# Block 1 of a four-block kernel: where the value matmuls stand, which engine makes a norm's products, and one beat for the next layer's features

## The chip, the cores and the metric

The kernel runs on one core of one Trainium2 chip. The metric is the device time of one execution, in microseconds. A profile adds the span from the first to the last instruction and the time of every instruction on each engine: PE (TensorE) for matmuls and transposes, ACT (ScalarE), DVE (VectorE), POOL (GpSimd), and SP, which issues the DMAs.

## What is computed

The program runs four blocks one after the other on an input of 2 batches x 1024 rows x 128 columns. The change touches only block 1, a two-layer attention block with two heads of 64:

```
def layer(x):                               # 2 layers; x: (2, 1024, 128)
    xl = ln(x) * g1 + b1
    q, k, v = xl @ wq + bq, xl @ wk + bk, xl @ wv + bv      # 2 heads of 64
    q, k = rotary(q), rotary(k)
    x = x + (softmax(q @ k.T / 8) @ v) @ wo
    hid = (ln(x) * g2 + b2) @ w1 + bias     # 128 -> 512
    return x + (hid * sigmoid(1.702 * hid)) @ w2
x = x0 + layers(layernorm(x0))
```

`ln` and `layernorm` take a row's mean and variance: (x - mean) / sqrt(var + 1e-5).

## The kernel before, in words

**Tiles.** Block 1 (class BlockA) works on tiles of 128 query rows: 2 layers x 2 batches x 8 tiles = 32 tiles. A tile is named here by its place in that order, 0 to 31. Four tiles make a group, and a group of 512 rows is the unit of the norms, the projection and the two-matmul feed-forward part.

**Beats.** The order of the work is written out by hand. Every tile has eight beats. A step is put down as "so many beats from now, at this rank"; when a beat comes, its steps run in order of rank and issue their instructions. Each engine takes its instructions strictly in the order in which they were issued. Steps of a chain are put down when the step before them has run; the ones with a set of allowed beats (EARLY is 1, 2, 3, 5 of the eight, LATE is 4, 5, 6, 7) take the first allowed beat that no such step has taken.

**A tile's own steps** (`tile`): the scores S at beat 0 (L372: eight matmul instructions into two wide PSUM tiles, then two maxima on DVE, L378); the two exponentials on ACT at beats 3 and 4 (L384); four groups of four transposes, T00, T10, T01, T11, at beats 9 to 12, that is beats 1 to 4 of the next tile (L395). ACT copies T00 and T10 out of PSUM (L398), DVE copies T01 and T11 (L400). The value matmuls come in two halves of 16 instructions, V0 at beat 13 and V1 at beat 15 (L407); `keep` at beat 16 copies their result on ACT (L415).

**A group's steps** (`after`, put down when the fourth tile is kept): the projection (L442) with two divisions on DVE (L450) and two additions on POOL (L454); a norm; `turn`, four transposes (L345) and one ACT copy with scale and bias, hT (L346); four `up` steps (L467, then tanh on ACT L470, a small POOL step L473 and, two beats later, a DVE step L475); two `down` steps (L488). In layer 0 a group then prepares layer 1 (`prep`): a norm, `features` (again four transposes, L345, and hT on ACT, L346), keys (L314, then ACT L316 and POOL L317), queries (L321, DVE L322) and values (L329, DVE L334).

**The norm** (`norm`) has two steps. `stats` at beat 0, 5 or 7, rank -2, is four pairs of DVE instructions (L289, L290). `product` one beat later, rank 0, is on POOL: add epsilon (L293), power -0.5 (L294), negate the mean (L295), and then four products (x - mean) * rs, one for each 128x128 tile (L297). For the very last group these four are on DVE. A norm is made 17 times by this function: four times for batch 1 at the start (two for the outer layernorm, two for layer 0), four times for layer 1, eight times in `after`, and once near the end for block 2.

**PSUM.** The two wide score tiles s0 and s1 take four of the eight banks. Everything else shares four banks, tag "bank": each group of transposes, the projection's two tiles, features, keys, queries, values, ups, downs, and the value matmuls' result u, which is held from V0 until `keep`.

**The order around the change.** In tile 10 (second group of batch 0, layer 0; the same order comes in tiles 14, 18 and 22) the steps that reach PE and ACT are, before the change:

```
tile 9,  beat 4: T11, PROJECT      beat 5: V0, features (next layer)   beat 7: V1
tile 10, beat 0: keep, product (POOL), S    beat 1: T00, keys   beat 2: T10
         beat 3: exp, T01    beat 4: exp, T11, queries   beat 5: V0, TURN
         beat 6: values      beat 7: V1, up0
```

The groups of tiles 6, 26 and 30 have a norm and a `turn` at the same beats, but no `prep` beside them.

Of the kernel before, what the change touches and what calls it, by code (L numbers as in the profile page):

```python
# [24 lines left out]
AF = mybir.ActivationFunctionType  # L25
ALU = mybir.AluOpType
# [82 lines left out]
class Pipe:  # L109
# [6 lines left out]
    def later(self, beats, f, bank=False, rank=0):  # L116
        at = self.now + beats
        if bank:
            among = range(1, 8) if bank is True else bank
            while at in self.taken or at % 8 not in among:  # L120
                at += 1
            self.taken.add(at)
        self.due.setdefault(at, []).append((rank, f))
# [54 lines left out]
class BlockA:  # L178
# [102 lines left out]
    def norm(self, src, dst, beats, eng=None):  # L281

        k, nc = self.k, self.k.nc
        st, mv, rs = self.small("st", [4, 6]), self.small("mv", [4, 2]), self.small("rs", [4])
        mn = self.small("mn", [4])

        def stats():
            for i in range(4):
                nc.vector.bn_stats(st[:, i, :], src[:, i, :])  # L289
                nc.vector.bn_aggr(mv[:, i, :], st[:, i, :])  # L290

        def product():
            nc.gpsimd.tensor_scalar(rs, mv[:, :, 1], 1e-5, None, ALU.add)  # L293
            nc.gpsimd.tensor_tensor(rs, rs, k.mhalf[:, :4], ALU.pow)  # L294
            nc.gpsimd.tensor_scalar(mn, mv[:, :, 0], -1.0, None, ALU.mult)  # L295
            for i in range(4):
                (eng or nc.gpsimd).tensor_scalar(  # L297
                    dst[:, i, :], src[:, i, :], mn[:, i : i + 1], rs[:, i : i + 1], ALU.add, ALU.mult
                )

        return (beats, (0, 5, 7), stats, -2), (1, False, product, 0)
# [46 lines left out]
    def prep(self, l, b, g):  # L348
        xn = self.p3.tile([P, 4, D], F32, tag="xn", name=self.k.name("xn"))
        features, keys, queries, values = self.linears(l, b, g, xn)  # L350
        return (
            *self.norm(self.x(b, g), xn, 1), (5, self.EARLY, features, 5), (2, self.EARLY, keys, 5),
            (1, self.LATE, queries, 5), (1, self.LATE, values, 5),
        )

    def tile(self, l, b, qt):
        k, nc = self.k, self.k.nc
        q, kk, v = self.q[b], self.kk[b], self.v[b]
        later = self.pipe.later
        g = qt // 4  # L360
        st = self.st.setdefault((l, b, g), {})
        cut = slice(qt % 4 * P, qt % 4 * P + P)
        t = {}

        def score():
            assert ("ready", l, b, 1) in self.st or (l, b) == (0, 0)
            t["s"] = [k.ps_a.tile([P, S], F32, tag=f"s{h}", name=k.name("s")) for h in range(2)]
            for j in range(2):
                for h in range(2):
                    rows = slice(h * 64, (h + 1) * 64)  # L370
                    keys = slice(j * 512, (j + 1) * 512)
                    nc.tensor.matmul(  # L372
                        t["s"][h][:, keys], q[rows, qt * P : (qt + 1) * P], kk[rows, keys],
                        start=True, stop=True,
                    )
            t["nm"] = [self.small("nm", [1]) for _ in range(2)]
            for h in range(2):
                nc.vector.tensor_reduce(t["nm"][h], t["s"][h], AX.X, ALU.max, negate=True)  # L378

        def exp(h):  # L380
            if qt % 4 == 0 and h == 0:
                st["sums"] = self.p2.tile([P, 2, 4], F32, tag="sums", bufs=3, name=k.name("sums"))
            t["pr", h] = self.p2.tile([P, S], F32, tag="pr", bufs=4, name=k.name("pr"))
            nc.scalar.activation(  # L384
                t["pr", h], t["s"][h], AF.Exp, bias=t["nm"][h],
                accum_out=st["sums"][:, h, qt % 4 : qt % 4 + 1],
            )

        def turn(h, j):
            if h == j == 0:  # L390
                t["pT"] = self.p2.tile([P, 2, MT, P], F32, tag="pT", name=k.name("pT"))
            ps = self.bank()
            for i in range(4):
                at = (j * 4 + i) * P
                nc.tensor.transpose(ps[:, i * P : (i + 1) * P], t["pr", h][:, at : at + P], k.ident)  # L395
            dst = t["pT"][:, h, j * 4 : j * 4 + 4].rearrange("p i q -> p (i q)")
            if j == 0:
                nc.scalar.copy(dst, ps)  # L398
            else:
                nc.vector.tensor_copy(dst, ps)  # L400

        def value(j):
            if j == 0:
                t["u"] = self.bank()
            for kb in range(j * 4, j * 4 + 4):
                for h in range(2):
                    nc.tensor.matmul(  # L407
                        t["u"][h * 64 : h * 64 + 64, :P], v[:, kb, h * 64 : h * 64 + 64],
                        t["pT"][:, h, kb], start=(kb == 0), stop=(kb == MT - 1),
                    )  # L410

        def keep():
            if qt % 4 == 0:
                st["us"] = self.p2.tile([P, 512], F32, tag="us", name=k.name("us"))
            nc.scalar.copy(st["us"][:, cut], t["u"][:, :P])  # L415
            if qt % 4 == 3:
                self.after(l, b, g, st)

        for at, rank, f in (
            (0, 0, score), (3, 0, lambda: exp(0)), (4, 0, lambda: exp(1)), (9, 2, lambda: turn(0, 0)),  # L420
            (10, 2, lambda: turn(1, 0)), (11, 2, lambda: turn(0, 1)), (12, 2, lambda: turn(1, 1)),
            (13, 2, lambda: value(0)), (15, 2, lambda: value(1)), (16, -3, keep),
        ):
            later(at, f, rank=rank)

# [1822 lines left out]
```

## Time and profile before

| what | us |
|---|---|
| median of 3 runs | 1286.3 (1286.21 to 1288.46) |
| the profiled execution | 1286.38 |
| its span, first to last instruction | 1284.6 |
| PE busy | 1147.2 (89%) |
| DVE busy | 874.7 (68%) |
| ACT busy | 645.9 (50%) |
| POOL busy | 488.7 (38%) |

Block 1 takes roughly the first 340 us. Times in the trace are microseconds from the span's start. A line of the timeline has the start, the duration, the engine, the source line and operation, what it writes and reads, how many instructions were merged, and in square brackets how long the engine was idle before it and what released it. "PEld" is the weight load that goes ahead of each matmul. "PEclk" is the clock that TensorE was granted, as a share of full speed.

### The profile page before, as it was taken

The page shows a single profiled execution, that of the slowest core. Times are in us where ns is not written, and L with a number is a line of the kernel's source. Part 1 is how long each engine was busy: PE and PEld are TensorE (multiplying, and loading weights), DVE is VectorE, ACT ScalarE, POOL GpSimd, SP SyncE. Part 2 cuts the span into 40 slices and gives each one's busy share as a digit, 9 for nine tenths or more (in the row PEclk, how much of TensorE's full clock was granted, in tenths as well). Part 3 has the DMA queues.
Part 4 walks back from the last instruction along what each step waited for, and adds up shares of the span by engine and source line. Part 5 has one row for each costly group of instructions (what it writes and reads, how often), then busy time and mean ns, then how long its engine had stood idle before and what let it go on. Part 6 is the DMA issues. An engine that isn't in the chain of part 4 may idle for free.

```text
span 1284.6 us, 23479 instructions
## 1 busy us (share of the span) xinstructions
PE 1147.2 (89%) x9441; PEld 744.3 (58%) x9441; DVE 874.7 (68%) x1782; ACT 645.9 (50%) x1216; POOL 488.7 (38%) x565
## 2 busy tenths in 40 slices
PE   5899999999688989989989877989999978997798
PEld 3566666666356656656656634545555543433688
DVE  5566666555587776776777525556577989999763
ACT  5455455444355665665664545656766754441000
POOL 1523333232588776676677442212222211100000
PEclk9999999999899999999999988989998999999799
DMA  9000000000010000010100011000000000000000
GB/s 296 3 1 1 1 1 1 2 1 1 18 26 22 22 22 18 22 26 18 26 22 18 5 50 69 2 1 2 2 1 1 2 1 1 0 17 1 26 17 17
DMA packets 19840, 25.18 MB, mean 20 GB/s; under 512 B 2762, under 2 KB 13716, under 8 KB 19476
## 3 DMA queue, kind: packets, MB, share of 16 engines
q1 hardware_dynamic: 19076, 23.02, 6.5%
q8 instruction: 75, 1.23, 0.4%
q10 hardware_dynamic: 656, 0.66, 0.2%
q14 instruction: 33, 0.27, 0.1%
HBM read 13.32 MB, written 1.05 MB: 11 GB/s over the span
## 4 chain that ended last, share of the span: by engine, by line
PE 60%; DVE 24%; ACT 7%; POOL 5%; issue 4%; DMA 0%; DVEq 0%; POOLq 0%; ACTq 0%
PE big L1667 6%; PE mm L1750 5%; PE bank L407 4%; PE s L372 4%; PE bank L962 4%; PE s L727 3%; PE bank L882 2%; PE s L1264 2%; PE s L837 2%; PE bank L467 2%; PE tr L1301 2%; PE s L1260 2%; DVE nm L1269 2%; PE bank L488 2%; DVE nm L378 2%
## 5 line engine op out<-in xcount | busy, mean ns | idle before, releaser
L1269 DVE TENSOR_REDUCE nm<-s 128x4 f32<-128x1024 f32 (+1 forms) x64 | 71.0, 1151 | 58.8 <-PE s L1264 58.5
L378 DVE TENSOR_REDUCE nm<-s 128x1 f32<-128x1024 f32 x64 | 75.1, 1215 | 51.9 <-PE s L372 51.9
L1302 ACT COPY pT<-tr 128x512 f32<-128x512 f32 x120 | 70.0, 598 | 71.8 <-PE tr L1301 71.6
L774 POOL TENSOR_TENSOR t<-raw,tab 128x512 f32<-128x512 f32 x62 | 77.2, 1267 | 74.4 <-DVE raw L765 74.4
L1301 PE MATMUL tr<-ident,pr 128*128 128x128 f32 x480 | 77.1, 284 | 2.6 <-ACT pT L1302 2.3
L736 ACT ACTIVATE sq<-s 128x1024 f32<-128x1024 f32 x32 | 32.8, 1023 | 87.0 <-PE s L727 87.0
L384 ACT ACTIVATE pr<-s,nm 128x1024 f32<-128x1024 f32 x64 | 71.0, 1120 | 7.9 <-DVE nm L378 7.8
L781 POOL TENSOR_TENSOR raw<-raw,tab 128x1024 f32<-128x1024 f32 x31 | 73.1, 2360 | 2.4
L788 POOL TENSOR_TENSOR raw<-raw,t 128x1024 f32<-128x1024 f32 x31 | 73.2, 2361 | 1.7
L395 PEld LDWEIGHTS bank<-ident,pr 128*128 128x128 f32 x512 | 56.2, 141 | 30.0 <-issue 22.5
L407 PE MATMUL bank<-pT,v 128*64 128x128 f32 x1024 | 72.5, 286 | 0.7 <-DVE pT L400 0.2
L1676 ACT ACTIVATE hid<-big,cols 128x512 f32<-128x512 f32 x62 | 41.9, 687 | 59.3 <-PE big L1667 59.3
L1667 PE MATMUL big<-xTd,d_gate 128*128 128x512 f32 x128 | 66.9, 611 | 5.0 <-DVE r_above L1917 2.5
L1667 PE MATMUL big<-xTd,d_up 128*128 128x512 f32 x128 | 68.5, 626 | 2.7 <-DVE r_above L1914 2.0
L407 PEld LDWEIGHTS bank<-pT,v 128*64 128x64 f32 x1024 | 57.2, 141 | 22.1 <-issue 10.8
L398 ACT COPY pT<-bank 128x512 f32<-128x512 f32 x64 | 34.9, 588 | 68.3 <-PE bank L395 68.3
L1301 PEld LDWEIGHTS tr<-ident,pr 128*128 128x128 f32 x480 | 54.6, 144 | 21.1 <-issue 11.7
L372 PE MATMUL s<-kk,q 64*128 64x512 f32 x256 | 64.7, 615 | 0.6 <-ACT pr L384 0.5
L395 PE MATMUL bank<-ident,pr 128*128 128x128 f32 x512 | 65.2, 276 | 0.0
L727 PE MATMUL s<-b_wqkv,hT 128*128 128x512 f32 x128 | 62.8, 613 | 1.7 <-ACT hT L694 1.3
L1750 PEld LDWEIGHTS mm<-d_down,hid 128*128 128x128 f32 x496 | 60.8, 195 | 5.7 <-DVE xo L1781 1.9
L1750 PE MATMUL mm<-d_down,hid 128*128 128x128 f32 x496 | 61.5, 279 | 1.3 <-DVE xo L1781 1.3
(368 smaller groups left out, 2833.8 us busy)
## 6 DMA issues: line engine op xcount, KB each, us to landing
vs<-v SPq DMA_DIRECT2D x60, 130.0 KB, 2.2
b_wqkv<-in_L_ffn_wqkv_dram SPq DMA_DIRECT2D x2, 768.0 KB, 9.4
b_tab<-in_c_xpos_dram SPq DMA_DIRECT2D x1, 1024.0 KB, 9.0
d_up<-in_L_ffn_Wup_dram SPq DMA_DIRECT2D x1, 1024.0 KB, 7.2
d_gate<-in_L_ffn_Wgate_dram SPq DMA_DIRECT2D x1, 1024.0 KB, 9.2
out_dram<-xo SPq DMA_DIRECT2D x3, 256.0 KB, 2.3
rows<-in_rows_dram SPq DMA_DIRECT2D x1, 760.0 KB, 6.6
b_w<-in_L_ffn_w_dram SPq DMA_DIRECT2D x2, 341.0 KB, 7.3
```

The source lines that it names most:

```text
L372: nc.tensor.matmul(t["s"][h][:, keys], q[rows, qt * P : (qt + 1) * P], kk[rows, keys], start=True, stop=True,)
L378: nc.vector.tensor_reduce(t["nm"][h], t["s"][h], AX.X, ALU.max, negate=True)
L395: nc.tensor.transpose(ps[:, i * P : (i + 1) * P], t["pr", h][:, at : at + P], k.ident)
L407: nc.tensor.matmul(t["u"][h * 64 : h * 64 + 64, :P], v[:, kb, h * 64 : h * 64 + 64], t["pT"][:, h, kb], start=(kb == 0), stop=(kb == MT - 1),)
L727: nc.tensor.matmul(qk[:, cut], lhsT, k.b_wqkv[:, l, cut], start=True, stop=True)
L774: nc.gpsimd.tensor_tensor(t2[:, :, :, a : a + 32], r4[:, :, :, z : z + 32], tab(1)[:, :, None, a : a + 32].to_broadcast([P, 2, 8, 32]), AL ...
L781: nc.gpsimd.tensor_tensor(r4, r4, tab(0)[:, :, None, :].to_broadcast([P, 2, 8, 64]), ALU.mult)
L788: eng.tensor_tensor(flat, flat, t["t2"].rearrange("p j h d -> p (j h d)"), ALU.add)
L1269: nc.vector.tensor_reduce(nm[h], view[h], AX.X, ALU.max, negate=True)
L1301: nc.tensor.transpose(ps[:, c * P : (c + 1) * P], pr[:, c, t * P : (t + 1) * P], k.ident)
L1667: self.k.nc.tensor.matmul(ps, weights[:, rows], self.xT[:, cut], start=True, stop=True)
L1750: nc.tensor.matmul(sums[part][:, cols], hid[tp, h, c][:, e, cols], k.d_down[:, c + 8 * e, :], start=start and e == 0, stop=False,)
```

## The change

Three edits, all in BlockA:

- In `norm`, `product` gets one more small POOL instruction, mr = -mean * rs. Two of the four products stay on POOL (or DVE for the last group), the other two become ACT instructions with scale rs and bias mr. They are issued in the same step, so at the same beat and rank.
- In `prep`, `features` is put down 6 beats behind the norm's product instead of 5.
- In `tile`, V0 and V1 move from beats 13 and 15 (rank 2) to beat 16, ranks -1 and -0.9. That is beat 0 of the tile after next, ahead of that tile's scores (rank 0). `keep` moves from beat 16 to beat 17, rank -3.

```
             nc.gpsimd.tensor_scalar(mn, mv[:, :, 0], -1.0, None, ALU.mult)
-            for i in range(4):
+            mr = self.small("mr", [4])
+            nc.gpsimd.tensor_tensor(mr, mn, rs, ALU.mult)
+            for i in range(2):
                 (eng or nc.gpsimd).tensor_scalar(
                     dst[:, i, :], src[:, i, :], mn[:, i : i + 1], rs[:, i : i + 1], ALU.add, ALU.mult
                 )
+            for i in range(2, 4):
+                nc.scalar.activation(
+                    dst[:, i, :], src[:, i, :], AF.Identity, bias=mr[:, i : i + 1], scale=rs[:, i : i + 1]
+                )
...
-            *self.norm(self.x(b, g), xn, 1), (5, self.EARLY, features, 5), (2, self.EARLY, keys, 5),
+            *self.norm(self.x(b, g), xn, 1), (6, self.EARLY, features, 5), (2, self.EARLY, keys, 5),
...
-            (13, 2, lambda: value(0)), (15, 2, lambda: value(1)), (16, -3, keep),
+            (16, -1, lambda: value(0)), (16, -0.9, lambda: value(1)), (17, -3, keep),
```

By the rule of the beats, the order in tile 10 becomes:

```
tile 9,  beat 4: T11, PROJECT
tile 10, beat 0: V0, V1 (of tile 8), product (POOL and ACT), S    beat 1: keep, T00, features
         beat 2: T10     beat 3: exp, T01, keys    beat 4: exp, T11, queries
         beat 5: TURN    beat 6: values            beat 7: up0
tile 11, beat 0: V0, V1 (of tile 9), S             beat 1: keep, ...
```

## The prediction

> **What bounds the kernel now.** I first read the windows of block 1, 37 us each, which is four tiles in the steady part. Columns: the stretch, its length, busy us of PE, PEld, DVE, ACT and POOL, granted clock, DMA.
>
> ```profile
> 58.00:95.00 37.00, 34.73 (x275) 22.65 (x274) 21.82 (x35) 18.71 (x37) 9.53 (x14) 0.95 0.00 1
> 132.00:169.00 37.00, 36.54 (x304) 25.01 (x304) 23.77 (x44) 19.27 (x36) 12.75 (x21) 1.00 0.01 2
> ```
>
> PE is busy 36.5 of 37 us and everything else has slack, so no reordering can win more than 0.5 us there; any PE stop is a loss. Only stretches like the first have something to win. The waits of PE from 18 to 322 us say where:
>
> ```profile
> PE bank L345 <- POOL xn L297: 6.9, 5, 1.5
> ```
>
> PE waits five times, 6.9 us in all, for a norm's products. The timeline shows one such place, tile 6:
>
> ```profile
> 73.13 1.07 ACT L398 COPY pT<-bank 128x512 f32<-128x512 f32 x2 [2.28 <-PE bank L395]
> ...
> 74.53 0.23 POOL L293 TENSOR_SCALAR rs<-mv 128x4 f32<-128x4 f32 x1 [1.82 <-DVE mv L290]
> ...
> 76.30 1.74 POOL L297 TENSOR_SCALAR xn<-xi,mn,rs 128x128 f32<-128x128 f32 x4
> ...
> 76.81 1.62 PE L345 MATMUL bank<-ident,xn 128*128 128x128 f32 x4 [1.43 <-POOL xn L297]
> ...
> 78.36 1.97 PE L407 MATMUL bank<-pT,v 128*64 128x128 f32 x16
> ...
> 82.04 1.99 PE L372 MATMUL s<-kk,q 64*128 64x512 f32 x8
> ```
>
> TURN waits 1.43 us; then V1 takes 1.97 us where 1.09 us is usual. The clock explains that: 0.59 and 0.56 from 78 to 82 us (windows of 2 us), 1.00 before and after.
>
> The steady case is tile 10:
>
> ```profile
> 107.73 0.78 ACT L346 ACTIVATE hT<-bank,cols 128x512 f32<-128x512 f32 x1 [0.81 <-PE bank L345]
> ...
> 110.57 0.66 PE L395 MATMUL bank<-ident,pr 128*128 128x128 f32 x4
> ...
> 111.32 0.59 ACT L398 COPY pT<-bank 128x512 f32<-128x512 f32 x1 [2.28 <-PE bank L395]
> ...
> 111.98 0.23 POOL L293 TENSOR_SCALAR rs<-mv 128x4 f32<-128x4 f32 x1 [1.82 <-DVE mv L290]
> ...
> 113.17 1.13 ACT L384 ACTIVATE pr<-s,nm 128x1024 f32<-128x1024 f32 x1
> ...
> 113.77 1.74 POOL L297 TENSOR_SCALAR xn<-xi,mn,rs 128x128 f32<-128x128 f32 x4
> ...
> 118.79 1.99 PE L372 MATMUL s<-kk,q 64*128 64x512 f32 x8
> ```
>
> While the norm is still in the making (POOL reaches its products at 113.77), ACT copies T00 at 111.32 and starts exponentials at 113.17. Tile 10 needs that ACT work at once.
>
> **The price of the new ACT products.** Block 2 already makes a norm this way, with the same POOL operations ahead:
>
> ```profile
> 352.03 0.23 POOL L657 TENSOR_SCALAR ln_rs<-ln_mv 128x4 f32<-128x4 f32 x1
> ...
> 353.77 0.20 POOL L660 TENSOR_TENSOR ln_mn<-ln_mn,ln_rs 128x4 f32<-128x4 f32 x1
> ...
> 354.01 1.65 ACT L664 ACTIVATE xi<-xo,ln_mn,ln_rs 128x128 f32<-128x128 f32 x4 [3.17 <-POOL ln_mn L660]
> ```
>
> So ACT starts 354.01 - 352.03 = 1.98 us after POOL's first step; four products take 1.65 us, start to start 0.39, one 0.48: two take 0.87. The bracket shows the point of the whole prediction: ACT sat idle 3.17 us in its queue until POOL was done.
>
> **ACT products, worked through tile 10.** They are issued at beat 0, ahead of tile 10's `keep`, T00 copy, hT, T10 copy and exponentials. POOL starts the norm at 111.98; it cannot start sooner, since projection, divisions and POOL additions ahead of it are not moved. ACT is free from about 108, and holds until 111.98 + 1.98 = 113.96. Its queue then runs (durations from the rows above, L415 0.27, L316 0.69, about 0.1 of overlap): products to 114.83, keep 115.0, T00 copy 115.5, hT 116.2, T10 copy 116.7, exp 117.9, keys 118.5, exp 119.6, TURN's hT from 119.6 to 120.4.
>
> PE meanwhile does S, T00, features, T10 until 112.1. Then all four banks are held: u (freed by keep), T00, features, T10, each by an ACT instruction behind the products. T01 waits until 115.0: a stop of 2.9 us where there was none. Keys, T11, queries, TURN and values follow with gaps to 120.2; up0 waits for hT, 120.5 to 121.5; V0 and V1 (1.02 each, of tile 9) to 123.55. Only then come the scores, at 123.55 instead of 118.79: **4.75 us**. In the tile before, the prep norm holds ACT too, but V0's move lets it begin 1 us sooner; the projection waits about 0.55 us, and the 0.5 us of features that left that tile pays for it. So tile 10's scores start where they did.
>
> A stop of 2.9 us and a thin stretch behind it may drop the clock as in tile 6, for some 4 us, of which waits on ACT cover most: 0 to 2.2 us more. I take 0.75, the low side, as PE mostly waits there: 5.5 us. Four groups (tiles 10, 14, 18, 22): **+22** (19 to 28).
>
> **Tiles 6, 26, 30.** POOL starts at 74.53, so ACT holds until 76.51, products to 77.4; keep 77.6, T00 copy 78.1, T10 copy 78.7, exponentials to 80.9, hT to 81.7. T11 finds no bank from 73.85 to about 77.4. Before, V0 and V1 stood ahead of TURN and of up0 and filled both waits; now nothing does: up0 starts at 81.75, V0 and V1 end at 84.85 at full clock, against scores at 82.04: +2.8. PE is nearly idle from 74 to 82, so the slow clock is likely: up0 +0.75 and V0 and V1 +0.95 each (up0 took 1.85, V1 1.97, above) make at most 5.5. I take 4.5: **+13.5** (8.4 to 16.5).
>
> **The start.** Product x10 holds ACT's first T00 copy from 30.0 to 31.9. Worse, prep's first norm waits on POOL behind the outer norm and the mask casts (L2059, L2064), till 41.89 in the trace, and its two ACT products now stand ahead of tile 2's copies, which ran at 36.01. ACT is held to about 43.4; V0 and V1 end near 47.8 and the scores of tile 3 come near 47.9 instead of 40.05. But PE lost time there already: waits for products at 44.17 and 47.77 (1.55 and 1.11 us, then four transposes in 1.62 us each), which go, as these are then ready. By tile 4's scores, 57.75 against 54.80, I have +3, and a slow clock in the 5 us hole adds 0 to 4: **+4.5** (2.5 to 8).
>
> **The rest.** Last group: DVE makes two products of 0.34 instead of four, ACT the others; the square of block 2's first tile (1.02, at 325.95, when ACT had nothing else) now stands behind them and delays hT by about 0.5: **+0.5** (0 to 1). Norm for block 2: POOL's products run at 285.32, ACT's next copy at 285.49 but the transposes' copies not before 288.04; nothing. The mr step, 0.20 on POOL: in the 1.98. POOL saves 0.87 a norm less 0.3: xn comes 0.5 us earlier at most. Features one beat later: 0.5 us of PE, moved (counted in tile 10). `keep` one beat later: this is what puts u's bank behind the products. V0 and V1 together: the same 32 instructions; beyond the lost filling they cost nothing in tiles 11 and 12, where ups and downs are queued without a gap (up3 waits for up1's bank instead of V0 for it). No DMA is issued by these steps.
>
> Sum: 22 + 13.5 + 4.5 + 0.5 = 40.5. The profiled execution took 1286.38 (span 1284.6 and 1.8 around it); the median is 1286.3, so nothing shifts: **1327 us**. Ends: 19 + 8.4 + 2.5 + 0 = 29.9 and 28 + 16.5 + 8 + 1 = 53.5, so 1316 to 1340.
>
> [...] Tile 6's row shows 0.59 after a wait of 1.43 us and slow transposes. [...]
>
> **Rivals.** (1) Only the bank stop counts: ACT's later backlog is swallowed by keys, queries and values, and the clock holds. Then 4 x 2.9, plus 3 x 0.7 (a 3.7 us stop less the 1.43 and 1.6 us lost now), plus 2.5 is 16: 1302. For it: ACT is busy 19.3 of 37 us. Against: up0 needs TURN's hT, last in that queue. (2) The clock stays low longer, and each late score delays the next exponentials: 8 a group, 6 a lone tile, 8 at the start: 59, about 1345. For it: long holes. Against: tile 6 recovered in 4 us. (3) Faster: ACT's wait falls in time it would idle anyway. Place: tiles 6, 26, 30, where xn comes 0.5 us sooner; if the stop gets short enough to keep the clock, 3 x (0.5 + 1.65) and 1 us at the start give 7.5: 1279. It decides if POOL has mr before T00's transposes end; in the rows it comes 2.8 us later (113.96 against 111.2). For it: ACT waits for PE 68 us at L398 in block 1. (4) The edits do not do what they say: no shorter wait and no held ACT, 1286.
>
> **Chances.** Forecast 0.64; (1) 0.15; (2) 0.12; (3) 0.07; (4) 0.02. The range 1300 to 1350 takes in (1) and (2) but for their tails and leaves out some 0.15 to 0.2. About 0.2% is what can be told from no change: faster 0.07, same 0.02, slower 0.91.
>
> **What would show it.** ACT's wait list gets "xn <- POOL mr" with several us each time; PE waits for banks released by ACT L415 and L398 in tiles 6, 10, 14, 18, 22, 26, 30; more windows with a clock under 1; the four-tile period grows from 36.7 us (tile 9's scores at 100.99, tile 13's at 137.73) to about 42; the rest of the program unchanged. I am wrong if ACT's products start without a wait, or if PE finds a bank in time.

## The result, and the profile after

Over six runs each the kernel takes 1324.05 us after the change (1321.38 to 1325.13) and 1287.2 before; the ratio is 1.0283, with a 95% interval of 1.0264 to 1.0301. It is slower by 36.9 us, the difference of the medians. The profiled execution after has a span of 1322.3 us, 37.7 more than before. Lines of `norm` and below are shifted by some six: what was L398 is L404, L415 is L421, L346 is L352, L372 is L378; ACT's new products are L303.

The waits in block 1 (columns: us in total, times, longest us). First those of PE, where before only the norm's products stood on top:

```profile
PE bank L401 <- ACT us L421: 29.9, 8, 5.8
PE bank L473 <- ACT hT L352: 9.3, 4, 2.6
```

PE no longer waits for POOL's products. It waits 29.9 us for a PSUM bank that `keep` (L421) frees, and 9.3 us for TURN's hT. Then those of ACT:

```profile
ACT xn L303 <- POOL mr L297: 83.1, 14, 7.1
ACT pT L404 <- PE bank L401: 38.2, 19, 2.3
```

ACT stands 83 us in front of its new products, until POOL has made mr. The timeline of tile 6 shows how one wait makes the other:

```profile
75.14 1.53 PE L401 MATMUL bank<-ident,pr 128*128 128x128 f32 x12
77.28 0.23 POOL L293 TENSOR_SCALAR rs<-mv 128x4 f32<-128x4 f32 x1 [1.82 <-DVE mv L290]
79.03 0.20 POOL L297 TENSOR_TENSOR mr<-mn,rs 128x4 f32<-128x4 f32 x1
79.27 0.88 ACT L303 ACTIVATE xn<-xi,mr,rs 128x128 f32<-128x128 f32 x2 [7.10 <-POOL mr L297]
80.06 0.24 ACT L421 COPY us<-bank 128x128 f32<-128x128 f32 x1
80.20 1.07 ACT L404 COPY pT<-bank 128x512 f32<-128x512 f32 x2
80.35 0.66 PE L401 MATMUL bank<-ident,pr 128*128 128x128 f32 x4 [3.68 <-ACT us L421]
83.34 0.80 ACT L352 ACTIVATE hT<-bank,cols 128x512 f32<-128x512 f32 x1
84.19 2.08 PE L473 MATMUL bank<-hT,a_w 128*128 128x512 f32 x2 [2.64 <-ACT hT L352]
86.20 3.17 PE L413 MATMUL bank<-pT,v 128*64 128x128 f32 x32
```

Twelve of the sixteen transposes run, then the four banks are taken. The last four start when `keep`, the first ACT instruction behind the products, has freed u. Then up0 waits for hT, the last in ACT's queue, and the 32 value matmuls, which filled such waits before, come behind it. More than half of them run slowly: 3.17 us, where 1.97 is usual for 32. The windows give the clock (the third figure from the end: the share granted):

```profile
82.00:84.00 2.00, 0.00 (x0) 0.00 (x0) 0.00 (x0) 2.00 (x5) 0.00 (x0) 0.50 0.00 0
84.00:86.00 2.00, 1.81 (x2) 0.50 (x2) 0.00 (x0) 0.14 (x1) 0.00 (x0) 0.50 0.00 0
86.00:88.00 2.00, 2.00 (x19) 1.80 (x20) 0.00 (x0) 0.69 (x1) 0.62 (x1) 0.50 0.00 0
88.00:90.00 2.00, 2.00 (x22) 1.59 (x20) 0.00 (x0) 0.27 (x1) 0.00 (x0) 0.83 0.00 0
```

Tile 10 begins the same way, but goes on differently:

```profile
117.73 0.60 PE L401 MATMUL bank<-ident,pr 128*128 128x128 f32 x4
118.53 0.23 POOL L293 TENSOR_SCALAR rs<-mv 128x4 f32<-128x4 f32 x1 [1.82 <-DVE mv L290]
120.53 0.88 ACT L303 ACTIVATE xn<-xi,mr,rs 128x128 f32<-128x128 f32 x2 [6.49 <-POOL mr L297]
121.32 0.24 ACT L421 COPY us<-bank 128x128 f32<-128x128 f32 x1
121.61 0.66 PE L401 MATMUL bank<-ident,pr 128*128 128x128 f32 x4 [3.28 <-ACT us L421]
121.94 0.78 ACT L352 ACTIVATE hT<-bank,cols 128x512 f32<-128x512 f32 x1
122.77 2.05 PE L320 MATMUL bank<-hT,a_wk 128*128 128x512 f32 x2 [0.51 <-ACT hT L352]
124.62 1.06 PE L401 MATMUL bank<-ident,pr 128*128 128x128 f32 x4
125.47 1.41 PE L327 MATMUL bank<-hT,a_wq 128*128 128x512 f32 x2
127.36 0.78 ACT L352 ACTIVATE hT<-bank,cols 128x512 f32<-128x512 f32 x1 [0.71 <-PE bank L351]
128.19 1.12 PE L473 MATMUL bank<-hT,a_w 128*128 128x512 f32 x2
```

ACT starts 120.53 - 118.53 = 2.00 us after POOL's first step, and PE stands 3.28 us for the bank. Then the clock falls (0.50 from 123 to 125 us): the keys take 2.05 us for 1.02, T11 1.06 for 0.60, the queries 1.41 for 1.02. ACT has caught up by then: it waits 0.71 us for TURN's transposes before it can make hT, and up0 at 128.19 starts without a wait.

Where the time came from is best seen in the starts of the tiles' scores (L372 before, L378 after), read from the timelines:

| scores of tile | before | after | difference |
|---|---|---|---|
| 4 | 54.80 | 57.90 | +3.10 |
| 6, 7 | 70.47, 82.04 | 73.22, 89.29 | +2.75, +7.25 |
| 10, 11 | 108.65, 118.79 | 114.88, 131.14 | +6.23, +12.35 |
| 14, 15 | 145.40, 155.53 | 156.72, 172.56 | +11.32, +17.03 |
| 18, 19 | 182.14, 192.28 | 198.14, 213.75 | +16.00, +21.47 |
| 22, 23 | 218.89, 229.03 | 239.33, 256.51 | +20.44, +27.48 |
| 26, 27 | 254.90, 266.42 | 281.69, 297.63 | +26.79, +31.21 |
| 30, 31 | 292.29, 303.90 | 322.81, 338.67 | +30.52, +34.77 |

Each of tiles 6, 10, 14, 18, 22, 26 and 30 loses 4 to 7 us, and nearly every tile between them gains about 0.34.

### The profile page after: what moved, and what is told of

The parts are those of the page before. It is cut to its first block, busy times and chain, and to the rows that moved or that the text cites. A ratio compares the mean times of both kernels' runs of the same rounds, so it can differ in the third digit from the quotient of the medians.

```text
span 1322.3 us, 23462 instructions
## 1 busy us (share of the span) xinstructions
PE 1152.6 (87%) x9441; PEld 754.4 (57%) x9441; DVE 875.5 (66%) x1780; ACT 656.1 (50%) x1250; POOL 478.0 (36%) x550
## 4 chain that ended last, share of the span: by engine, by line
PE 58%; DVE 25%; ACT 9%; POOL 4%; issue 4%; DMA 0%; DVEq 0%; ACTq 0%; POOLq 0%
PE big L1673 6%; PE mm L1756 4%; PE bank L413 4%; PE bank L968 3%; PE s L378 3%; DVE nm L384 3%; PE s L733 3%; PE bank L888 2%; PE s L1270 2%; PE s L843 2%; PE s L1266 2%; PE bank L473 2%; PE tr L1307 2%; DVE nm L1275 2%; PE bank L494 2%
## 5 line engine op out<-in xcount | busy, mean ns | idle before, releaser
L401 PE MATMUL bank<-ident,pr 128*128 128x128 f32 x512 | 71.2, 285 | 29.9 <-ACT us L421 29.9
L413 PEld LDWEIGHTS bank<-pT,v 128*64 128x64 f32 x1024 | 59.9, 145 | 17.2 <-DVE pT L406 6.1
L413 PE MATMUL bank<-pT,v 128*64 128x128 f32 x1024 | 67.8, 288 | 1.4 <-ACT pT L404 1.1
L378 PE MATMUL s<-kk,q 64*128 64x512 f32 x256 | 65.0, 615 | 0.6 <-ACT pr L390 0.5
L1279 ACT ACTIVATE pr<-s,nm 128x256 f32<-128x256 f32 (+1 forms) x160 | 60.9, 470 | 1.9 <-DVE nm L1275 1.5
```

What stands on the lines that cost most here:

```text
L378: nc.tensor.matmul(t["s"][h][:, keys], q[rows, qt * P : (qt + 1) * P], kk[rows, keys], start=True, stop=True,)
L413: nc.tensor.matmul(t["u"][h * 64 : h * 64 + 64, :P], v[:, kb, h * 64 : h * 64 + 64], t["pT"][:, h, kb], start=(kb == 0), stop=(kb == MT - 1),)
```

## The experiments

Theory: ACT takes its instructions in order (in tile 10 `keep`, whose value matmuls end at about 114.9 us, runs at 121.32, behind the products), so the products hold it until POOL has mr, and PE runs out of banks and operands behind it. Rival: moving the values away from where they filled waits is the loss. "At tile 31" below is the difference from before at that tile's scores, +34.8 for the changed kernel; it leaves out what blocks 2 to 4 add.

**The norm's edit alone.**

```
 before.py
+            mr = self.small("mr", [4])
+            nc.gpsimd.tensor_tensor(mr, mn, rs, ALU.mult)
-            for i in range(4):                       # all on POOL
+            for i in range(2):                       # and i = 2, 3 on ACT, as in the change
```

> The kernel before, with the norm's edit alone (mr on POOL, two of four products on ACT at the same beat and rank). Theory (ACT is held in its queue until POOL has mr, and PE runs out of banks): slower, but less than with all three edits, because keep still stands ahead of the products and V0 and V1 still fill PE's waits: about 3 us a combined group, 1.2 us a lone tile, 3 us at the start, 0.5 at the end, 1305 us (1298 to 1315), with some 70 to 90 us of ACT waiting for POOL mr. Rival (the loss comes from moving the values away from where they filled waits, and ACT's wait falls in time that it would idle): 1284 to 1290.

Measured: 1306.7 us, ratio 1.0159 (1.012 to 1.0197); at tile 31 +20.7. PE's waits:

```profile
PE bank L413 <- ACT pT L404: 17.4, 5, 5.6
PE bank L401 <- ACT pT L404: 6.3, 4, 1.6
```

ACT's wait for mr is 50.6 us, less than the 70 to 90 expected. The theory's time holds, the rival falls: the hold alone costs 18 us or more, and V0 (L413) now waits for copies behind the products.

**The values alone, the features alone, and both.**

```
 before.py                                        (values)
-            (13, 2, lambda: value(0)), (15, 2, lambda: value(1)), (16, -3, keep),
+            (16, -1, lambda: value(0)), (16, -0.9, lambda: value(1)), (17, -3, keep),
 before.py                                        (features)
-            (5, self.EARLY, features, 5)
+            (6, self.EARLY, features, 5)
```

> The kernel before, with V0, V1 and keep moved alone. Theory (the loss is the held ACT): within 4 us of before, 1283 to 1291: 0.34 us gained in most of the 28 tiles, since the 32 value matmuls run in one piece, against 1 to 2 us lost in each tile where TURN waits for the norm and V0 no longer fills that wait. No wait of ACT for POOL. Rival (the values' place is the loss): 1300 or more.

> The kernel before, with the next layer's features one beat later alone. Both the theory and the rival: 0.5 us of PE work moved over the scores, nothing else, 1286 us within 2.

> The changed kernel with the norm of before (four products on POOL, no mr): values and features moved alone. Theory: all of the loss is gone, 1280 to 1289, a little below the run with the values alone, as features fill 0.5 us of TURN's wait in four tiles. Rival (the values' place is the loss): 1300 or more.

Measured: values alone 1289.4, ratio 1.0031 (1.0012 to 1.0051), at tile 31 +6.0. Features alone 1285.9, ratio 0.9982 (0.9962 to 1.0002), at tile 31 -3.0. Both 1292.9, ratio 1.0047 (1.003 to 1.0063), at tile 31 +4.4. Both is 3.9 us above its range: I had priced the lost filling at 1 to 2 us a tile, and the values alone lose 2.9 us from tile 6 to 7 and again from 26 to 27. The wait in the kernel with the values alone is

```profile
75.26 1.62 PE L345 MATMUL bank<-ident,xn 128*128 128x128 f32 x4 [2.46 <-POOL xn L297]
```

2.46 us where it was 1.43, because V0's 1.02 us no longer stands in it. Still, without ACT's products the other edits make up 4.4 of 34.8 us.

The -3.0 us of the features alone is not a gain in the groups that the prediction had in view. By the starts of the scores the move wins 2.2 us at the start of the block (tile 3 to 4, where a second wait for the norm goes) and 1.6 us each in tiles 6 and 26, where it moves nothing; in tile 6 the clock now stays up (last section). In the groups of tiles 10, 14, 18 and 22 it costs 0.6 us each.

**The wait or the work?** First the same ACT instructions in the same place, on data that is always there:

```
 after.py
-   bias=mr[:, i : i + 1], scale=rs[:, i : i + 1]
+   bias=k.eps, scale=k.col("a_g1", 0)
```

> The changed kernel, but ACT's two products take their bias and scale from constants that are there from the start, so this kernel leaves out the normalisation of half the tiles; place and work of the ACT instructions are the same, only the wait for POOL's mr goes. Theory (it is the wait): ACT starts the products when x is ready, some 3.7 us sooner in tile 10, ahead of T00's transposes, and nearly all the loss goes: 1281 to 1292. Rival (it is the added work on ACT, 15 norms of two instructions, and the banks): 1310 or more.

Measured: 1283.8, ratio 0.9978 (0.9959 to 0.9997); at tile 31 +0.3. In its tile 10 the products start as soon as x is ready:

```profile
106.83 0.88 ACT L303 ACTIVATE xn<-xi,eps,cols 128x128 f32<-128x128 f32 x2 [3.26 <-POOL xi L460]
108.61 0.23 POOL L293 TENSOR_SCALAR rs<-mv 128x4 f32<-128x4 f32 x1 [1.82 <-DVE mv L290]
```

They are done before POOL has begun the norm, and the loss is gone: it is the wait. The run may flatter the edit: half of the products are ready sooner here than real data would allow, and at tile 31 it is 4.1 us below the kernel with both other edits and no ACT products. Then twice the work:

```
 after.py
-            for i in range(2): (POOL)    for i in range(2, 4): (ACT)
+                                         for i in range(4): (ACT)
```

> The changed kernel with all four products on ACT and none on POOL. Theory (the wait for mr is the cost, the ACT work a small one): every ACT instruction behind the products comes 0.78 us later in some 14 norms, 8 to 12 us more, 1332 to 1336; the wait of ACT for mr stays about 90 us. Rival (ACT's work is the cost): it doubles, and so does the loss, 1355 or more.

Measured: 1327.6, ratio 1.0305 (1.0281 to 1.0328). At tile 31 it is +44.0, 9.2 us above the changed kernel; twice the work adds a quarter to the loss, so the rival falls. The whole is only 3.5 above and under the expected 1332 to 1336, because blocks 2 to 4 differ (last section). ACT's wait for mr is 76.9 us in all, for 83.1 in the changed kernel and 90 expected.

**Which instruction behind the products?** `keep` ahead of them:

```
 after.py
-            (17, -3, keep),
+            (16, -0.8, keep),
```

> The changed kernel with keep at beat 16, rank -0.8: behind V1 but ahead of the ACT products, so u's bank is freed before ACT is held. Theory A (ACT's copies and exponentials behind the products set the time; the bank that PE names is only the first to come free): T01 moves up, but keys, hT and up0 stay where they are: 2 to 4 us less, 1320 to 1322. Theory B (u's bank, held by keep, is what stops PE, as the waits on L421 of 29.9 us say): 20 us or more less, 1304 or below.

Measured: 1324.9, ratio 1.0284 (1.0261 to 1.0307), at tile 31 +35.3: no gain at all. Its PE waits:

```profile
PE bank L320 <- ACT hT L352: 16.1, 4, 4.0
PE bank L351 <- ACT pT L404: 7.3, 2, 3.7
PE bank L413 <- ACT pT L404: 6.8, 2, 5.6
```

The wait for u's bank is gone and others of the same size stand in its place, the largest for the features' hT, which the keys need. Theory B falls. Theory A's account fits, the work behind the products sets the time, but the 2 to 4 us that it promised did not come.

**Norm and features, values where they were.**

```
 before.py, with the norm's edit and
-            (5, self.EARLY, features, 5)
+            (6, self.EARLY, features, 5)
```

> The kernel before with the norm's edit and the later features, the values left where they were. Theory (ACT's hold costs half by itself, and the other half comes because V0 and V1 no longer fill PE while hT is late): 1303 to 1309, like the norm's edit alone (1306.7), so some 17 us of the change's 36 belong to the pair. Rival (the hold makes up the whole 36 us once features stand where they do in the changed kernel): 1318 or more.

Measured: 1318.0, ratio 1.0246 (1.0232 to 1.026); at tile 31 +30.9. My theory for the second half fell: with the norm's edit in place, it is mostly the features, not the values. Tile 10 shows why:

```profile
118.78 0.88 ACT L303 ACTIVATE xn<-xi,mr,rs 128x128 f32<-128x128 f32 x2 [4.83 <-POOL mr L297]
119.56 0.56 ACT L404 COPY pT<-bank 128x512 f32<-128x512 f32 x1
120.03 0.77 ACT L352 ACTIVATE hT<-bank,cols 128x512 f32<-128x512 f32 x1
120.86 1.13 PE L320 MATMUL bank<-hT,a_wk 128*128 128x512 f32 x2 [3.40 <-ACT hT L352]
```

With the norm's edit alone, features' hT is made in the tile before, ahead of the products; one beat later it stands behind them, and the keys wait 3.4 us. So a move that takes 3.0 us off by itself adds 10.2 (from +20.7 to +30.9) beside the hold. Part of that is the clock: the move adds 1.4 us in the group of tile 10, where the clock stays at 1.00, and 2.8 to 3.0 in each of those of tiles 14, 18 and 22, where it falls (0.50 from 164 to 166 us in tile 14, where the queries take 1.92 us) and with the norm's edit alone does not (queries 1.12 us). The values add 3.8 more: 2.9 in tiles 6 and 26 each, 1.8 in tile 30 and 2.0 in tile 10, less what they win in the tiles between. These shares hold for this order of the edits; the norm's edit with the values and without the features was not run.

**ACT's products where mr is ready.**

```
 after.py, ACT's loop moved into
+            def late(): ...
+            self.pipe.later(3, late, rank=0.5)
```

> The changed kernel with ACT's two products issued three beats behind POOL's steps, at rank 0.5: in a tile with a norm's product at beat 0 that is just behind its first exponential, where mr is there. Same work, same engines. Theory: ACT no longer waits for POOL and the loss goes: 1278 to 1287, possibly below before, as TURN's operand comes 0.5 us sooner and the values run in one piece. Rival (the split of the norm itself is the loss): 1310 or more.

Measured: 1297.9, ratio 1.006 (1.003 to 1.009); at tile 31 +11.1. The expectation was missed by 11 us. ACT's wait for mr is gone in the tiles with a TURN, but PE waits

```profile
PE bank L355 <- POOL xn L299: 10.0, 7, 2.6
PE bank L477 <- ACT hT L356: 8.0, 7, 1.4
```

With the products ahead of the second exponential, TURN's hT comes later, and with the values gone from there nothing fills the time before up0. At the start of the block three beats are not enough, and ACT is still held:

```profile
43.09 0.88 ACT L305 ACTIVATE xn<-xi,mr,rs 128x128 f32<-128x128 f32 x2 [3.34 <-POOL mr L297]
45.12 3.78 PE L382 MATMUL s<-kk,q 64*128 64x512 f32 x6 [2.70 <-ACT pr L394]
```

The second exponential stands behind these products, and tile 3's scores wait 2.70 us for it. The kernel with both other edits and no ACT products is 5 us faster in all; at tile 31 it is 6.6 us ahead, 4.9 of them already at tile 4's scores.

**A version that beats both kernels.** The values are put together only in tiles without a TURN; then the features' edit is added; then ACT's late products.

```
 before.py
+        if qt % 4 == 1:
+            late = ((13, 2, lambda: value(0)), (15, 2, lambda: value(1)), (16, -3, keep))
+        else:
+            late = ((16, -1, lambda: value(0)), (16, -0.9, lambda: value(1)), (17, -3, keep))
...
-            (13, 2, lambda: value(0)), (15, 2, lambda: value(1)), (16, -3, keep),
+            *late,
```

> The kernel before with the values together only where no TURN stands in the tile: V0, V1 and keep of the second tile of each group stay at beats 13, 15 and 16, the others go to 16, 16 and 17. Norm as before. Theory: the 0.34 us a tile are kept in some 20 tiles and the losses of the tiles with a TURN go: 5 to 8 us less in block 1, 1279 to 1284 in all. Rival (the gain of 0.34 us a tile is lost again at the next wait): 1286 to 1289.

> As the run with the values together in the free tiles, and the features one beat later. Theory: features alone took 3 us off block 1, so 1277 to 1283. Rival (features and values fill the same waits): as without, 1280 to 1284.

> As the run with values in the free tiles and later features, and the norm's two ACT products issued three beats behind POOL's steps. Theory: no hold of ACT, V0 fills TURN's wait, TURN's operand complete about 0.8 us sooner in three lone tiles: within 3 us of the run without it, 1275 to 1283. Rival (ACT's two more instructions delay the second exponential and the scores behind it): 3 to 8 us more than the run without it.

Measured: 1277.6, ratio 0.9933 (0.992 to 0.9946), at tile 31 -6.4; with features 1277.0, ratio 0.9925 (0.9911 to 0.9938), at tile 31 -9.0; with late ACT products 1278.0, ratio 0.9943 (0.9931 to 0.9955), at tile 31 -5.6. The intervals do not tell this last run from the one without ACT's products, but block 1 does: it is 3.4 us longer, all of it before tile 4's scores, where ACT is held as in the run before (3.32 us for mr). The second exponential comes late there, as the rival had it, though by the wait and not by the work. So the values' edit is good where no wait has to be filled. The split norm brings nothing between tiles 4 and 31, where it holds nobody, and costs at the start, where it does. The 2.6 us that the features win in block 1 come, as with the features alone, from the start (2.0) and from a clock that stays up in tiles 6 and 26 (V1 1.09 us in each, for 1.97 and 1.98; 1.6 each), less 0.6 in each of the four groups; the whole shows too little of them to settle. Tile 7 shows the gain of 0.35 us; first before, then the version:

```profile
87.20 1.13 PE L467 MATMUL bank<-hT,a_w 128*128 128x512 f32 x2 [0.41 <-DVE hid L475]
88.26 1.09 PE L407 MATMUL bank<-pT,v 128*64 128x128 f32 x16
89.28 1.13 PE L467 MATMUL bank<-hT,a_w 128*128 128x512 f32 x2
90.34 1.09 PE L407 MATMUL bank<-pT,v 128*64 128x128 f32 x16
```

```profile
85.44 1.98 PE L471 MATMUL bank<-hT,a_w 128*128 128x512 f32 x4 [0.41 <-DVE hid L479]
87.35 1.97 PE L407 MATMUL bank<-pT,v 128*64 128x128 f32 x32
89.25 1.13 PE L372 MATMUL s<-kk,q 64*128 64x512 f32 x4
```

The same instructions take 4.16 us (87.20 to the scores at 91.36) in four runs, and 3.81 us (85.44 to 89.25) in two.

## Why the prediction was right, point by point

- **The hold.** Right: ACT's longest wait in block 1 is "xn <- POOL mr". The 1.98 us from POOL's first step were 1.99 (tile 6) and 2.00 (tile 10); two products 0.88 for 0.87.
- **Tiles 10, 14, 18, 22.** 22 predicted; 6.1 + 5.7 + 5.5 + 7.0 = 24.3. The bank stop was right (3.28 us for 2.9), the path behind it was not. The prediction let ACT's queue run on to TURN's hT and up0 wait for it; in the trace ACT had caught up and waited 0.71 us for PE, and up0 did not wait. In its place the clock took more than the 0.75 us allowed: keys, T11 and queries took 1.9 us longer than usual. Two errors of opposite sign, so that this term fits is in part luck. The clock fell (0.50 from 123 to 125 us) after a stop of 3.28 us.
- **Tiles 6, 26, 30.** 13.5 predicted; 4.5 + 4.4 + 4.3 = 13.2. Here the path is the one worked out: the bank stop (3.68 us), then up0's wait for hT (2.64 us), then up0 and the values at the slow clock (0.50 from 82 to 88 us in tile 6, from 292 to 296 in tile 26, from 333 to 337 in tile 30).
- **The start.** 4.5 predicted, 3.1 at tile 4. The slow clock (0.50 from 42 to 46 us, 0.57 to 48) cost what was allowed for it: T01 took 1.12 us for 0.66 and the 32 value matmuls 3.12 for 1.97, 1.6 us together, where 1.5 stands in the sum. So the +3 at full clock was about twice what came.
- **The end.** +0.5 predicted; block 2's second projection is at +34.6, so between tile 31 and there it is -0.2, perhaps because the values of tiles 30 and 31 run in one piece there too.
- **V0 and V1 together "cost nothing" in other tiles.** Wrong in sign: they gain about 0.34 a tile, and the tiles outside the terms above make -5.8 (34.8 - 3.1 - 13.2 - 24.3 = -5.8). With them falls the reading that no reordering can win more than 0.5 us in a four-tile period because PE is busy 36.5 of 37 us: with the values together in the free tiles, the period from tile 10 to 14 is 36.05 us, 0.7 less than before.
- **"The rest of the program unchanged".** Its code is, its time is not: +3.1 from block 2's second projection on.
- **The sum.** The terms that were priced measured 24.3 + 13.2 + 3.1 - 0.2 = 40.4, against 40.5. That the total agrees so well is luck, since they are off by +2.3, -0.3, -1.4 and -0.7; the two that were not priced, -5.8 and +3.1, bring it to 37.7.
- **The named stop.** The prediction put 2.9 us on the banks, and PE's list agrees, but the run with `keep` first shows that u's bank was not the cause by itself: freed, it uncovers the hT of features behind it.
- **Rival (1)** had one half right: in tiles 10, 14, 18 and 22 ACT's later backlog was swallowed. The clock did not hold, and up0 did wait in tiles 6, 26 and 30.
- **Rival (2)** put 8 us on a group, 6 on a lone tile and 8 on the start; they measured 6.1, 4.4 and 3.1.
- **Rival (3)**, the faster end, did not come. Its condition was that POOL has mr before T00's transposes end; in tile 10 they end at 117.45 us and mr is there at 120.50. Even with the wait cut out, block 1 is 0.3 us longer at tile 31.

## What to carry to other kernels

On an engine that works in order, an instruction costs the time from when the engine could have started it to when its operand is there, and everything issued behind it pays (here ACT stood 83.1 us in front of its products; with constants in place of mr, tile 31 came at +0.3 us and not at +34.8): before moving work to an idle engine, look at what is ready first, that operand or the instructions behind it. The wait that the profile names is only the first to come free; freeing it alone may show the next one of the same size (29.9 us at u's bank, then 16.1 + 7.3 + 6.8 = 30.2 at three others). An edit that looks harmless alone (features, -3.0 us) can cost much together with a hold (+10.2), so their effects are not to be added up.

## What the runs showed of the hardware that was not expected

**The same stall drops the clock in one run and not in another.** In tile 6 TURN waits 1.43 us for the norm and its four transposes take 1.62 us, in the kernel before and in the one with the features alone. Before, the clock falls behind it (0.59 and 0.56 from 78 to 82 us, in windows of 2 us). With the features alone, where the same stall comes 2.2 us earlier, it does not:

```profile
74.66 1.62 PE L345 MATMUL bank<-ident,xn 128*128 128x128 f32 x4 [1.43 <-POOL xn L297]
76.00:78.00 2.00, 2.00 (x19) 1.23 (x19) 0.00 (x0) 0.78 (x1) 0.00 (x0) 1.00 0.00 0
78.00:80.00 2.00, 2.00 (x9) 0.69 (x8) 0.00 (x0) 0.84 (x2) 0.62 (x1) 1.00 0.00 0
```

All windows from 70 to 90 us show 1.00 there, and V1 takes 1.09 us for 1.97. The code of tile 6 is the same, and the tile takes 9.97 us for 11.57. Tile 26 is 1.6 us shorter in that run too. In the version with the features V1 stands behind the same stall three times: 1.43 us in tile 6, 1.41 in tile 26 and 1.43 in tile 30. It takes 1.09 us in the first two and 1.59 in the third.

Blocks 2 to 4 are the same in all kernels, yet from the second projection of block 2 to the end they took 3.1 us more than before in the changed kernel (+34.6 there, +37.7 in all), 5.1 less in the one with four ACT products (+45.4, +40.3) and 3.0 less with the values alone (+5.1, +2.1). One place in block 3 shows half of the 3.1, with the same instructions in the same order, before and after:

```profile
992.00:994.00 2.00, 2.00 (x12) 1.26 (x8) 1.23 (x4) 0.19 (x1) 2.00 (x4) 0.72 0.00 0
994.00:996.00 2.00, 2.00 (x29) 1.30 (x28) 1.69 (x2) 0.16 (x1) 0.80 (x1) 1.00 0.00 0
```

```profile
1027.00:1029.00 2.00, 2.00 (x7) 0.80 (x6) 1.34 (x3) 0.00 (x0) 2.00 (x3) 0.50 0.00 0
1029.00:1031.00 2.00, 2.00 (x17) 1.22 (x16) 0.30 (x1) 0.00 (x0) 0.15 (x1) 0.56 0.00 0
```

The clock came back at about 993 before; after, it stayed at half until about 1031, and the difference grew there from 34.36 to 35.93 us. Why the clock came back later there is not shown, and neither is why the stall of tile 6 counts in one run and not in another. An edit of a quarter of a per cent in one block can be hidden by such shifts (3.1 of 1287.2 us here).

**In tile 7 four short runs of matmuls of two kinds took longer than two long ones:** 4.16 us before and 3.81 in the version, 0.35 us for two changes of kind fewer. What in TensorE takes that time is not shown.
